# Diagonal of the attention matrix: VectorE sums and two transfers in place of products with ones on TensorE

## The chip, the cores and the metric

The kernel runs on one core of a Trainium2 chip. The engines named below are TensorE (PE; its weight loads are listed apart as PEld), VectorE (DVE), ScalarE (ACT), GpSimd (POOL) and SyncE (SP), whose queue issues the transfers. The metric is the device time of one execution in microseconds (us); the time of a version is the median of its runs.

## The reference

Input x has 32 batches of 512 nodes with 128 features; adj is a 512 x 512 matrix, mostly zeros. Four graph layers follow each other, each as x = x + layer(relu(layernorm(x)), adj). Only the first layer is touched:

```
h0 = h @ W[0];  h1 = h @ W[1]
m  = adj > 0
A  = softmax(where(m, e[cumsum(m) - 1], -9e15), axis=1)      # 512 x 512
M  = eye(512)
out = (A * M) @ h0 + (A * (1 - M)) @ h1 + bias
```

So the attention matrix A is split into its diagonal, which scales the rows of h before a product with W[0], and the rest, which multiplies h W[1]. The layers behind it (two Chebyshev hops, a message layer, a dense attention) only take part as the work that fills the rest of the time.

## The kernel before, in words

The 512 nodes lie as NT = 4 tiles of 128 partitions. The order of the instructions on PE, DVE, ACT and POOL is written out by hand: from line 166 to line 1148 they run in source order on each engine. Transfers on SP are placed by the tile framework, except where the source asks for program order. Within an engine, an instruction that waits holds up all those behind it.

The opening stage, some 40 us, builds A row tile by row tile (t = 0 to 3). `score_rows(t)` makes the scores on PE (lines 625 and 629). `softmax_rows(t)` adds and minimises them on DVE (636, 637) and exponentiates on ACT (638), `inverse(t)` takes the reciprocal on DVE (642), and `scaled_rows(t)` writes the scaled row tile into `att` on ACT (645). The columns inside a row tile are stored in a crossed order (32-wide pieces), which `split` and `crossed` undo. Of each row tile, the 128 x 128 block on the diagonal is called `own`. POOL multiplies it by the identity into `diag` (648) and subtracts that from `own` (649), so `att` holds A without its diagonal.

PE then transposes `att` (line 475) into four PSUM banks `p_attT`; ACT and DVE copy them out in halves (line 316), and `att_sums` builds from them, on DVE, the sums of a Strassen-like scheme of seven half-size products (lines 331 to 335). The right operands are `g`, the projected h W[1] (PE 435, copies 460), and its differences `rt_g`, made on POOL (356).

`round0(r)` does the first layer for two pairs of batches, r = 0 to 7. It runs the seven products on PE (line 386, banks p_l_a, p_l_c, p_l_d) and does other work between them: statistics on DVE (227, 233, 235, 236), normalisation on ACT (247), transposes of h (265, copies 268), later done by DVE and transfers (283, 290, 292). The diagonal part is added by `straight_block` (line 759), which multiplies `hd` by W[0] into the same banks. `hd` is made on POOL by `straight` (line 703): the feature-major h times `adiag`, a 128 x 512 tile whose every partition holds the 512 diagonal values, so that a column scaling becomes an elementwise product.

`adiag` is made once, in round 0 after the second product: `ones`, a 128 x 128 tile of ones, multiplies `diag` on PE, tile by tile (828), which sums each column of `diag` over partitions and leaves the sum on every partition; ACT copies the bank out (829). `adiag` stays in use for the whole first layer.

Of the kernel before, what the change touches and what calls it, by code (L numbers as in the profile page):

```python
# [9 lines left out]
F32 = mybir.dt.float32  # L10
# [14 lines left out]
def kernel(  # L25
# [51 lines left out]
    def bank(name):  # L77
        return psum.tile([P, 512], F32, tag="bank", name=name)
# [11 lines left out]
    def crossed(ap):  # L90

        return ap.rearrange("p (a b c) -> p b a c", a=NT, b=NQR)

    def split(ap):
        return ap.rearrange("p (a b c) -> p a b c", a=NT, b=NQR)
# [83 lines left out]
    nc.scalar.activation(prep.tile([P, 1], F32, name="powers"), eps, AF.Exp)  # L179
    minus_half = const.tile([P, NT, 2], F32, name="minus_half")  # L180
    nc.vector.memset(minus_half, -0.5)
    ones = const.tile([P, P], F32, name="ones")
    nc.vector.memset(ones, 1.0)

    known = prep.tile([P, NT, 2], F16, name="known")
    nc.vector.tensor_copy(known[:, :, 1], rows)
# [280 lines left out]
    def go(steps, n=99):  # L467
        for _ in range(n):
            if next(steps, steps) is steps:
                return  # L470
# [145 lines left out]


    diag = prep.tile([P, NT, P], F32, name="diag")
    least = prep.tile([P, NT], F32, name="least")
    total = prep.tile([P, NT], F32, name="total")  # L620

# [19 lines left out]
    def inverse(t):  # L641
        nc.vector.reciprocal(total[:, t : t + 1], total[:, t : t + 1])

    def scaled_rows(t):
        nc.scalar.mul(split(att[:, t, :]), crossed(us[t]), total[:, t : t + 1])
        own = split(att[:, t, :])[:, :, t, :]
        d = diag[:, t, :].rearrange("p (b c) -> p b c", c=QR)
        nc.gpsimd.tensor_mul(d, own, ident.rearrange("p (b c) -> p b c", c=QR))
        nc.gpsimd.tensor_sub(own, own, d)

    attT = square_tile("attT")
# [12 lines left out]
    softmax_rows(2)  # L664
    inverse(1)
    scaled_rows(1)
    score_rows(3)
    next(turned[1])
    next(turned[1])
    softmax_rows(3)  # L670
    inverse(2)
    scaled_rows(2)
    go(early_stats_2, 2)
    inverse(3)
    scaled_rows(3)
    next(project[1])
    pt = [bank(f"p_attT_{j}") for j in range(NT)]
    transpose_rows(pt, att, 0)
    transpose_rows(pt, att, 1)
    go(project[1])  # L680
    left_of_att = att_sums()
    next(left_of_att)
    att_copies((0, 0, nc.scalar.copy), (1, 0, nc.vector.tensor_copy),
# [37 lines left out]

    ahead = {q: stats_steps(q) for q in range(4, NQ)}
    ln3 = stats_steps(3)
    own, turning, hd, adiag = {}, {}, {}, []
    sums_ahead = late_sums()

    def normalise(q):
# [34 lines left out]
    def round0(r):  # L762

        now = rights.pop(r)
        if r == 0:

            adiag.append(work.tile([P, N], F32, tag="rt", name="adiag", bufs=6))
            p_adiag = bank("p_adiag")  # L770
        A, C = 2 * r, 2 * r + 1

        def x_of(I, b):
            return x_block(r, I, b)

        def diagonal(p, I, b, first):
            straight_block(p, lambda w: hd[A + w, b], I, w0[:, 0, :], first)

        u = [u_tile(f"l0_{r}_{i}") for i in range(3)]
        held = {}  # L780

        def evict(k, p):
            pv = halves(p)
            if k == 1:
                nc.vector.tensor_add(tiles(u[0].rearrange("p i e -> p (i e)")), tiles(p), spread(b0, NT))
            elif k == 6:
                nc.vector.tensor_add(u[1], pv, u[0])
            elif k == 5:
                held["d"] = pv
            elif k == 7:  # L790
                nc.vector.tensor_add(u[2], pv, u[0])
                nc.vector.tensor_add(u[2], held["d"], u[2])
            elif k == 2 and r == 0:
                held["a"] = p
            elif k == 2:
                upper(p)
            elif k == 4:
                diagonal(p, 1, 0, False)
                nc.vector.tensor_add(x_of(1, 0), of_pairs(pv), x_of(1, 0))
            elif k == 3:  # L800
                diagonal(p, 0, 1, False)
                nc.vector.tensor_add(x_of(0, 1), of_pairs(pv), x_of(0, 1))

        def upper(p):
            diagonal(p, 0, 0, False)
            nc.vector.tensor_add(x_of(0, 0), of_pairs(halves(p)), x_of(0, 0))

        def add(I, b, i):
            nc.gpsimd.tensor_add(x_of(I, b), x_of(I, b), of_pairs(u[i]))

        more = r + 1 < NQ // 2
        nothing = iter(())
        stats_a, stats_c = ahead.get(A + 5, nothing), ahead.get(C + 5, nothing)
        own_a, own_c = own.pop(A - 2, nothing), own.pop(C - 2, nothing)
        for i, _ in enumerate(products(f"l0_{r}", by_token, sums["att"], now, evict,
                                          ORDER if r else ORDER0)):
            if r == 0:
                if i == 0:
                    transpose_rows(pt, att, 2)
                    transpose_rows(pt, att, 3)  # L820
                    att_copies((0, 1, nc.scalar.copy), (1, 1, nc.vector.tensor_copy))
                    next(left_of_att)
                    next(left_of_att)
                    go(early_stats_2)
                    att_copies((2, 1, nc.scalar.copy), (3, 1, nc.scalar.copy))
                elif i == 1:
                    for t in range(NT):
                        nc.tensor.matmul(p_adiag[:, blk(t)], ones, diag[:, t, :], start=True, stop=True)
                    nc.scalar.copy(adiag[0], p_adiag)  # L829
                    go(normal[2], NT + 1)  # L830
                    diagonal_of(0, 0)
                    go(ln3, NT + 1)
                    go(normal[2])
                    next(left_of_att)
                    next(left_of_att)
                    next(squares)
                    go(ln3)
                elif i == 2:
                    diagonal_of(0, 1)
                    add(1, 0, 0)  # L840
                elif i == 3:
                    next(turned[2])
                    go(turned[2])
                    add(0, 1, 1)
                    bias(0)
                    normalise(3)
                    go(ahead[4], NT)
                    go(squares)
                elif i == 4:
                    upper(held["a"])  # L850
                    turned.append(pe_steps(h[3], "hT0_3", hT[3]))
                    next(turned[3])
                    go(ahead[4])
                    add(1, 1, 2)
                    go(turned[3])
                    go(projection(2))
                    normalise(4)
                    go(ahead[5], NT)
                    bias(1)
                    go(turn(4))  # L860
                    go(ahead[5])
                elif i == 5:
                    go(projection(3))
                    go(right_of(1))
                    diagonal_of(1, 0)
                    normalise(5)
                elif i == 6:
                    go(stats_c, NT)
                continue
            if i == 0:  # L870
                if C + 2 < NQ:
                    go(turn(C + 2))
                if A + 4 < NQ:
                    normalise(A + 4)
                diagonal_of(r, 1)
                add(1, 0, 0)
            elif i == 1:
                add(0, 1, 1)
                go(stats_a, NT + 1)
                go(own_a, NT)  # L880
                if more:
                    bias(r + 1)
                go(stats_a)
                go(own_a)
            elif i == 2:
                if more:
                    go(projection(A + 2))
            elif i == 3:
                add(1, 1, 2)
                if not more:  # L890
                    next(next_layer)
                if C + 4 < NQ:
                    normalise(C + 4)
                if r >= 3:
                    go(sums_ahead, 2)
            elif i == 4:
                if A + 4 < NQ:
                    go(turn(A + 4))
            elif i == 5:
                if more:  # L900
                    go(projection(C + 2))
                    go(right_of(r + 1))
                    diagonal_of(r + 1, 0)
                go(stats_c, NT + 1)
                go(own_c, NT)
            elif i == 6:
                go(stats_c)
        p = bank(f"p_l0_{r}_e")
        diagonal(p, 1, 1, True)
        nc.vector.tensor_add(x_of(1, 1), of_pairs(halves(p)), x_of(1, 1))  # L910
        if r == 0:
            go(stats_c)
        go(own_c)
        own[A], own[C] = stats_steps(A), stats_steps(C)
        if r + NQ // 4 < NQ // 2:
            loads(r + NQ // 4)
# [279 lines left out]
```

## Time and profile before

| | |
|---|---|
| time, median of 3 runs | 964.42 us (964.27 to 965.08) |
| profiled span | 962.7 us |
| PE busy | 953.7 us |
| DVE, ACT, POOL busy | 585.3, 470.1, 421.7 us |
| products with ones, line 828 | 8 instructions of 275 ns, starting from 34.2 to 34.9 us |
| copy of adiag, line 829 | 587 ns, at 35.3 us |
| POOL product and difference of the diagonal, 648 and 649 | 4 of 459 ns and 4 of 457 ns, from 24.7 to 30.1 us |
| first use of adiag, line 703 | POOL, at 35.9 us |

The page of a profile lists busy time by engine, then the chain of work that ended last, followed back from the last instruction through whatever released each step. A row of the timeline gives the start, the duration, the engine, the line, the operation with its output and inputs, a count, and in brackets how long the engine had been idle and what ended that. A row of the chain gives the start, the duration on the chain and the piece of work. Names carry no buffer numbers.

### The profile page before, as it was taken

How to read it: one execution, taken by the hardware profiler on the slowest of the kernel's cores; microseconds unless marked ns; L12 is line 12 of the kernel's file. 1: busy time of each engine (PE TensorE's matmuls, PEld its weight loads, DVE VectorE, ACT ScalarE, POOL GpSimd, SP SyncE). 2: the span in 40 equal slices, each digit the busy share in tenths (PEclk: the TensorE clock that was granted, in tenths of full speed). 3: DMA queues.
4: the chain of work that ended last, by engine and by line, in shares of the span. 5: the costliest groups of instructions: out<-in, count | busy, mean ns of one | idle time of the engine just before them, and what ended most of it. 6: DMA issues, size and time to landing. Idle time of an engine off the chain costs nothing.

```text
span 962.7 us, 15161 instructions
## 1 busy us (share of the span) xinstructions
PE 953.7 (99%) x5469; PEld 780.9 (81%) x5469; DVE 585.3 (61%) x1332; ACT 470.1 (49%) x1055; POOL 421.7 (44%) x463
## 2 busy tenths in 40 slices
PE   8999999999999999999999999999999999999998
PEld 4899999898989989899878777777677777767776
DVE  8878885846536546657667665665654444444444
ACT  5865452442232233277627654444765445544553
POOL 4878987833517522512333444433032233223322
PEclk9999999999999999999999999999999999999999
DMA  9256533341341231343333423233131121211111
GB/s 253 60 157 192 155 110 88 95 114 55 104 138 41 70 84 27 110 110 92 85 105 99 127 88 88 70 86 88 55 89 55 55 77 44 76 57 45 55 33 44
DMA packets 83913, 86.04 MB, mean 89 GB/s; under 512 B 6784, under 2 KB 74624, under 8 KB 83840
## 3 DMA queue, kind: packets, MB, share of 16 engines
q1 hardware_dynamic: 83840, 85.09, 31.8%
q8 instruction: 43, 0.70, 0.3%
q14 instruction: 30, 0.25, 0.1%
HBM read 44.17 MB, written 40.89 MB: 88 GB/s over the span
## 4 chain that ended last, share of the span: by engine, by line
PE 96%; ACT 2%; DMA 1%; DVE 1%; SPq 0%; issue 0%; DVEq 0%; ACTq 0%
PE p_av L1116 12%; PE p_score L1101 11%; PE p_l_c L386 8%; PE p_w L435 6%; PE p_l_d L386 5%; PE p_msgT_c L379 5%; PE p_l_a L386 4%; PE p_x1T_c L379 4%; PE p_l L435 3%; PE p_feat L435 3%; PE p_hv L435 3%; PE p_msgT_d L379 3%; PE p_msgT_a L379 3%; PE p_phi L1071 3%; PE p_qkh L1088 3%; PE p_phi L1072 3%
## 5 line engine op out<-in xcount | busy, mean ns | idle before, releaser
L247 ACT ACTIVATE h<-x,sh,rs 128x128 f32<-128x128 f32 x512 | 209.6, 488 | 51.2 <-PE p_x1T_d L379 21.7
L1106 POOL TENSOR_TENSOR ex<-ex,adjTx 128x512 f32<-128x512 f32 x62 | 80.5, 1298 | 208.1 <-ACT ex L1104 208.1
L1102 ACT ACTIVATE ex<-p_score 128x512 f32<-128x512 f32 x128 | 71.9, 587 | 122.8 <-issue 113.0
L1116 PEld LDWEIGHTS p_av<-qkh_hv,ex 128*128 128x128 f32 x1024 | 118.4, 191 | 8.4 <-issue 7.4
L1116 PE MATMUL p_av<-qkh_hv,ex 128*128 128x129 f32 x1024 | 119.9, 274 | 0.0
L1101 PE MATMUL p_score<-qkh_hv,hT 128*128 128x512 f32 x256 | 115.2, 593 | 0.0
L283 DVE STREAM_TRANSPOSE hb_hT<-h 128x512 f32<-128x512 f32 x120 | 82.0, 698 | 23.7 <-ACT h L247 23.4
L1106 DVE TENSOR_TENSOR ex<-ex,adjTx 128x512 f32<-128x512 f32 x66 | 46.2, 703 | 81.7 <-ACT ex L1104 81.7
L227 DVE BATCH_NORM_STATS2 bn<-x 128x6 f32<-128x256 f32 x248 | 89.7, 417 | 0.6
L1101 PEld LDWEIGHTS p_score<-qkh_hv,hT 128*128 128x128 f32 x256 | 46.2, 190 | 46.5 <-issue 44.7
L1104 ACT ACTIVATE ex<-ex 128x512 f32<-128x512 f32 x128 | 76.7, 630 | 1.9
L356 POOL TENSOR_TENSOR rt_feat<-feat,feat 128x256 f32<-128x256 f32 x16 | 11.6, 727 | 136.0 <-ACT feat L1055 136.0
L949 ACT COPY w<-p_w 128x512 f32<-128x512 f32 x32 | 18.3, 577 | 106.0 <-PE p_w L435 106.0
L356 POOL TENSOR_TENSOR rt_w<-w,rt_w 128x512 f32<-128x512 f32 x16 | 20.4, 1276 | 110.4 <-DVE rt_w L356 92.1
L435 PE MATMUL p_w<-th,x1T 128*128 128x128 f32 x256 | 49.5, 275 | 0.0
L435 PE MATMUL p_w<-th,hs 128*128 128x128 f32 x256 | 49.5, 275 | 0.0
L435 PEld LDWEIGHTS p_hv<-vw,hT 128*128 128x128 f32 x256 | 33.6, 192 | 15.3 <-issue 8.1
L1066 POOL TENSOR_TENSOR x<-x,phi2b 128x256 f32<-128x256 f32 x64 | 44.5, 730 | 0.0
L435 PEld LDWEIGHTS p_w<-th,hs 128*128 128x128 f32 x256 | 39.9, 192 | 0.7
L1055 ACT ACTIVATE feat<-feat 128x512 f32<-128x512 f32 x32 | 20.2, 632 | 41.3 <-DVE feat L1054 41.3
L1121 DVE SCALAR_TENSOR_TENSOR x<-p_av,rsum,x 128x128 f32<-128x128 f32 x128 | 39.1, 347 | 1.9
L703 POOL TENSOR_TENSOR hd<-hT,adiag 128x512 f32<-128x512 f32 x32 | 39.7, 1275 | 0.3 <-ACT adiag L829 0.3
(234 smaller groups left out, 2039.0 us busy)
## 6 DMA issues: line engine op xcount, KB each, us to landing
d_hT<-hb_hT SPq DMA_DIRECT2D x240, 128.0 KB
hT<-d_hT SPq DMA_DIRECT2D x60, 512.0 KB
x<-in_x_dram SPq DMA_DIRECT2D x32, 256.0 KB
out_dram<-x SPq DMA_DIRECT2D x31, 256.0 KB
adj_s<-in_adj_dram SPq DMA_DIRECT2D x4, 256.0 KB
adjT_d<-adj_squares SPq DMA_DIRECT2D x4, 256.0 KB
sq<-in_adj_dram SPq DMA_DIRECT2D x4, 256.0 KB
adjTx<-adjT_d SPq DMA_DIRECT2D x4, 256.0 KB
```

The source lines that it names most:

```text
L227: nc.vector.bn_stats(st[:, k].rearrange("p e s -> p (e s)"), xt[q][:, b, t : t + 2, :].rearrange("p t f -> p f t"))
L247: nc.scalar.activation(h[:, b, t, :], xt[q][:, b, t, :], AF.Relu, bias=shift[q][:, i : i + 1], scale=scale[q][:, i : i + 1])
L283: nc.vector.transpose(hb[:, :, b].rearrange("p j t r -> p t j r"), h[:, b].rearrange("p t (j c) -> p t j c", c=QR))
L379: nc.tensor.matmul(p[:, :H], b[:, k, :], a[:, k, :], start=(first and k == 0), stop=(k == 1), skip_group_check=True)
L386: nc.tensor.matmul(p[:, i * 2 * D : (i + 1) * 2 * D], a[:, k, blk(i)], b[:, k], start=(first and i == 0 and k == 0), stop=(k == 1), skip_g ...
L435: nc.tensor.matmul(p[:, blk(t)], hT(t), w, start=(i == 0), stop=(i == len(terms) - 1))
L1066: tc.keep_in_program_order(nc.gpsimd.tensor_add(xi, xi, spread(phi2b, 2)))
L1101: nc.tensor.matmul(ps, hT[:, t, b, :], qkh, start=True, stop=True)
L1102: nc.scalar.activation(ex[:, t, :], ps, AF.Tanh, scale=1.0 / (8.0 * math.sqrt(D)))
L1104: nc.scalar.activation(ex[:, t, :], ex[:, t, :], AF.Exp, scale=8.0)
L1106: eng.tensor_mul(split(ex[:, t, :]), split(ex[:, t, :]), crossed(adjTx[0][:, t, :]))
L1116: nc.tensor.matmul(po[:, i, : D + 1], ex[:, t, blk(i0 + i)], hv[:, t, :], start=(t == 0), stop=(t == NT - 1))
```

## The change

The diagonal values are now taken by DVE. A fused multiply and reduce over the free dimension writes `diag` (own times identity) and, in the same instruction, its row sum, which is the diagonal element of that row, into one column of `diag_of` (128 x 4). POOL keeps only the subtraction. The four calls are spread through the opening stage as `without_diagonal(t)`. A first transfer writes `diag_of` to 512 consecutive words in DRAM, a second reads those words back to all 128 partitions as `adiag`. Both stand in program order on SP, before the attT copies. PE's products with ones, the bank they used, ACT's copy and the `ones` tile are gone. `adiag` is allocated earlier, ahead of the `rt_g` tiles of round 0. The aim is to take work from PE and ACT that other parts of the chip can do.

```
-    ones = const.tile([P, P], F32, name="ones")
-    nc.vector.memset(ones, 1.0)
...
+    diag_of = prep.tile([P, NT], F32, name="diag_of")
...
     def scaled_rows(t):
         nc.scalar.mul(split(att[:, t, :]), crossed(us[t]), total[:, t : t + 1])
+
+    def without_diagonal(t):
+
         own = split(att[:, t, :])[:, :, t, :]
         d = diag[:, t, :].rearrange("p (b c) -> p b c", c=QR)
-        nc.gpsimd.tensor_mul(d, own, ident.rearrange("p (b c) -> p b c", c=QR))
+        nc.vector.tensor_tensor_reduce(d, own, ident.rearrange("p (b c) -> p b c", c=QR), 1.0, 0.0,
+                                       OP.mult, OP.add, diag_of[:, t : t + 1])
         nc.gpsimd.tensor_sub(own, own, d)
...
     softmax_rows(2)
     inverse(1)
     scaled_rows(1)
+    without_diagonal(0)
     score_rows(3)
...
     softmax_rows(3)
+    without_diagonal(1)
     inverse(2)
     scaled_rows(2)
     go(early_stats_2, 2)
     inverse(3)
     scaled_rows(3)
     next(project[1])
+    without_diagonal(2)
     pt = [bank(f"p_attT_{j}") for j in range(NT)]
     transpose_rows(pt, att, 0)
     transpose_rows(pt, att, 1)
-    go(project[1])
+    next(project[1])
+    without_diagonal(3)
+    next(project[1])
+
+    adiag = [work.tile([P, N], F32, tag="rt", name="adiag", bufs=6)]
+    diag_d = bounce.tile([N], F32, tag="diag", name="diag_d", bufs=1)
+    tc.keep_in_program_order(nc.sync.dma_start(diag_d.rearrange("(t p) -> p t", p=P), diag_of))
+    tc.keep_in_program_order(nc.sync.dma_start(
+        adiag[0], bass.AP(tensor=diag_d.tensor, offset=diag_d.offset, ap=[[0, P], [1, N]])))
     left_of_att = att_sums()
...
-        if r == 0:
-
-            adiag.append(work.tile([P, N], F32, tag="rt", name="adiag", bufs=6))
-            p_adiag = bank("p_adiag")
...
                 elif i == 1:
-                    for t in range(NT):
-                        nc.tensor.matmul(p_adiag[:, blk(t)], ones, diag[:, t, :], start=True, stop=True)
-                    nc.scalar.copy(adiag[0], p_adiag)
                     go(normal[2], NT + 1)
```

More of the change, by code (lines that the diff above doesn't have):

```diff
@@ L723 @@
     ln3 = stats_steps(3)
-    own, turning, hd, adiag = {}, {}, {}, []
+    own, turning, hd = {}, {}, {}
     sums_ahead = late_sums()
```

## The prediction

> **What bounds the kernel now.** I read the page first: engines, then the chain.
>
> ```profile
> PE 953.7 (99%) x5469; PEld 780.9 (81%) x5469; DVE 585.3 (61%) x1332; ACT 470.1 (49%) x1055; POOL 421.7 (44%) x463
> ...
> PE 96%; ACT 2%; DMA 1%; DVE 1%; SPq 0%; issue 0%; DVEq 0%; ACTq 0%
> ```
>
> TensorE is busy for 99% of the span and holds 96% of the chain that ended last. Every operation that the diff touches lies, by the view of the tile diag, between 24.7 and 35.3 us (its products with ones at 34.2, their copy at 35.26), apart from the readers of adiag, which begin at 35.9. So only a stretch of some twenty microseconds matters, and what comes out of it shifts all the rest. The chain of waits in time order shows that stretch:
>
> ```profile
> 27.93 1.23 ACT att L645 x2
> 29.16 0.36 ACT attT L316
> 29.52 0.04 issue
> 29.56 1.99 PE p_l_a L386 x8
> 31.55 0.87 PE p_attT L475 x8
> 32.43 1.90 PE p_l_a L386 x8
> 34.33 0.91 PE p_adiag L828 x8
> 35.24 0.02 issue
> 35.26 0.02 ACT adiag L829
> 35.28 0.46 issue
> 35.74 2.04 ACT h L247 x5
> ...
> 40.23 3.09 ACT h L247 x8
> 43.32 0.04 issue
> 43.36 0.33 PE p_hT L265
> 43.69 1.79 PE p_g L435 x16
> ```
>
> See two things. The products with ones are on the chain (0.91 us), and so is the copy behind them: ACT begins the third normalisation at 35.74 because of it. From 35.74 to 43.3 the chain is ACT, not PE; from 43.36 on it is PE without a gap until 181 us. The result is therefore the shift of the moment 43.36, carried to the end. The timeline of DVE shows what stands where the new instructions go:
>
> ```profile
> 27.96 0.16 DVE L642 RECIPROCAL total<-total 128x1 f32<-128x1 f32 x1
> 28.05 1.27 DVE L460 COPY g<-p_g 128x512 f32<-128x512 f32 x2
> 29.25 0.42 DVE L316 COPY attT<-p_attT 128x256 f32<-128x256 f32 x1
> 29.59 0.75 DVE L227 BATCH_NORM_STATS2 bn<-x 128x6 f32<-128x256 f32 x2
> ```
>
> DVE has no gap here, and its attT copy ends at 29.67, when PE's first p_l_a products, started at 29.56, come to need it (their second instruction pair reads the block that DVE copies).
>
> [...] the reduce of line 637 shows 0.69 us, [...] the four d_hT transfers issued from 50.08 show data from about 50.8 to 53.3, and the dependent issue begins at 53.98. No row of before shows a transfer of 4-byte elements that I can time.
>
> **The change, part by part.**
>
> Removed from PE: 8 instructions of p_adiag, 0.91 us on the chain. Removed from ACT: one copy of 0.59 us and a wait of 1.52 us before it. Without them ACT's next instruction waits for sh of line 236, which ends at 34.42 in the old trace, 1.32 us before 35.74. The ones memset (0.17 us at 0.9) is followed by a wait for POOL's rows, so it was hidden. POOL loses 4 products of 0.46 us; these lie beside other work, since its rt_g operations also wait for DVE's copies of g (ended 29.32).
>
> Added to DVE: four reduces with their accumulator reads. By start-to-start times of line 637 (22.25, read at 22.87, next at 22.94) overlap takes 0.07 us off and the read adds 0.07, so I take 0.29 us each, bounded by 0.22 (read free) and 0.6 (as slow as the 512-wide one).
> - Row 0 stands behind the reciprocal of 24.43 and waits for ACT's att (ends 24.58). It pushes the hT copy from 24.65 to 24.91 and the score operation to 25.52, which ends at 26.2; the next reduce waits for PE until 26.38 anyway. The idle 0.38 us there hides it.
> - Row 1 moves inverse(2) from 27.00 to about 27.4; ACT wants it at 27.84 behind its exponential. Hidden.
> - The two statistics and inverse(3) then end at 28.28, ahead of ACT's fourth row at 28.45. Hidden.
> - Row 2 needs att row 2, which ACT ends at 28.56. DVE waits from 28.3 to 28.58 and goes on at 28.87; behind it stand the first copy of g (0.6, to 29.47), row 3 (to 29.76; its att ended at 29.16), the second copy of g (to 30.36), and the attT copy, which ends at 30.78 in place of 29.67: 1.11 us later. That is the price.
>
> PE begins p_l_a at 29.56 as before, does two instructions, waits until 30.82, and does the other six at 0.216 us (1.73 for 8): it ends at 32.12, and the transposes begin then in place of 31.39: +0.73. Everything behind carries +0.73 on PE and DVE until the p_adiag slot, where 0.89 us (start to start, 34.17 to 35.06) is saved: p_l_c begins at 34.90 in place of 35.06, the next transposes (38.52 before) at 38.36. PE gains 0.16.
>
> ACT: sh of line 236 ends at 34.42 + 0.73 = 35.15, so normalisation starts at 35.17 in place of 35.74, and its eight instructions and the square root (its statistics end at 36.5, in time) end at 38.57. The copies of hT need PE's first four transposes, 38.36 + 0.5 = 38.86 (before, 39.15, ACT-bound); the second follows at 39.36, and the next normalisation begins at 39.88 in place of 40.11 to 40.23, ending 0.25 us earlier. With it 43.36 becomes about 43.1. **Sum: -0.25 us.**
>
> Added transfers: SP issues nothing between 24.8 and 41.65 us, and all 16 engines idle from about 28 to 42, so nothing is queued behind. The first waits for row 3's read at 29.85. From the d_hT row: 0.8 us from issue to data, 0.65 from last data to the next issue. 512 pieces of 1 KB took 2.5 us there, so for 512 pieces of 4 bytes I take 0.6 to 2.5, say 1.5. The second: 0.8 to data, 256 KB at 180 to 350 GB/s (rates seen at d_hT) 0.7 to 1.4[...]. adiag lands at 29.95 + 0.8 + 1.5 + 0.65 + 0.8 + 1.1 + 0.5 = 35.3, between 34.3 and 36.6. POOL ends its rt_g work at about 35.7 and reaches hd then (35.92 before), so the wait is at most about 0.9 us. Who waits: PE's p_l_a L759 at 41.1 needs the first two hd (2.5 us after the start, slack 2.7), and behind hd stand POOL's additions, whose last frees DVE at 44.63, then ACT's normalisation at 45.99, then its copies of g (end 50.5) and POOL's rt_g (second ends 53.2), wanted by PE at 55.12: slack about 2 us. A landing up to 37.8 costs nothing.
>
> **The rivals.**
> 1. All of PE's share is gained: the reduces pair away without moving the attT copy, as their low bound and some slack would allow. Then PE is 0.89 us earlier, ACT starts at 34.44: about 0.9 saved, 963.5. For it: PE is 96% of the chain. Against: DVE shows no gap from 27.0 to 30.95.
> 2. The reduces cost about 0.6 each: the first two spill past the idle 0.38 us by some 0.5, the last two push the copy by 0.6 more; 43.36 moves by about +0.9, 965.3. For it: this is a custom operation whose 128-wide form the trace lacks.
> 3. The new wait is the transfers: 4-byte writes at three times the 1 KB pieces' time, so that adiag lands near 40.2. Then 2.4 us lie beyond the slack and, as the path is in order from POOL to PE, come through, less the 0.25: 966.6. For it: 512 scattered elements. Against: 512 larger pieces took 2.5 us.
>
> **How the numbers follow.** The forecast (shift of -0.25, from 964.42 to 964.2) gets 0.58, rival 1 0.19, rival 2 0.12, rival 3 0.08; 0.03 is left for an effect late in the kernel in my favour. The bound of 0.2% is 1.93 us: the forecast and rivals 1 and 2 lie within it, rival 3 outside. PE's whole saving of 0.9 with its stalls between 28 and 43 us (1.73 + 1.73 + 3 x 0.87 or so of work in 8.3 us of chain leave about 0.5, and 0.3 near 29.3) is under 1.93, so faster beyond it is nearly shut out: faster 0.04, same 0.86, slower 0.10. The range takes in rivals 1 and 2: 963.1 to 965.6.
>
> **What would show it.** In the profile after: PE has 8 matmuls fewer; line 316's DVE copy starts near 30.4, and PE shows a wait of about 0.8 us inside the first p_l_a; ACT has no wait of 1.5 near 35; its normalisation starts near 35.2; POOL's first hd starts within 0.5 us of 35.9, and PE's p_g (43.5 before) stands near 43.3 in the same count. If PE's first p_l_a runs through, rival 1 holds; if the reduce rows read 0.5 us or more, rival 2; if POOL waits for adiag beyond 38, rival 3. The prediction is wrong if a wait appears after 45 us that has no row in the old trace, since everything rests on the shift being carried unchanged.

## The result, and the profile after

The change makes the kernel slower: 972.26 us (971.60 to 973.05, 6 runs) against 964.35 us, a ratio of 1.0081 (95% interval 1.0068 to 1.0094), 7.9 us more. The forecast was 964.2, with a range up to 965.6. Of the cases that the prediction worked out, the one that came true is rival 3, given a chance of 0.08, and it came in more than three times as large as it was worked out.

Line numbers after the change differ by -2 to +14. The page of the changed kernel first: engines, the row of the granted TensorE clock, the chain by engine.

```profile
PE 956.3 (99%) x5461; PEld 782.4 (81%) x5461; DVE 586.8 (61%) x1339; ACT 469.3 (48%) x1054; POOL 419.4 (43%) x459
...
PEclk9899999999999999999999999999999999999999
...
PE 93%; DVE 3%; DMA 2%; ACT 1%; issue 0%; SPq 0%; POOL 0%; DVEq 0%; ACTq 0%
```

PE has its 8 matmuls fewer and yet 2.6 us more busy time; one slice of the clock row is under 9. The totals say no more. The waits do: first those of SP's queue up to 60 us, then those of the engines from 20 to 70 us (who waited, for what; us in total, times, longest).

```profile
SPq L693 <- DMA diag_d<-diag_of: 10.0, 1, 10.0
```

```profile
DVE x L816 <- POOL x L443: 8.8, 1, 8.8
POOL hd L717 <- DMA adiag<-diag_d: 8.2, 1, 8.2
...
PEld p_l_a L773 <- POOL hd L717: 4.3, 2, 3.6
PE p_l_a L773 <- POOL hd L717: 3.6, 2, 3.2
```

The whole line of causes is there. SP waits 10.0 us for the 2 KB write before it may issue the spread; POOL waits 8.2 us for adiag, and what stands behind hd in its order comes later with it (the additions of u at 48.26, before at 40.86); PE waits 3.6 us for hd, and DVE 8.8 for POOL's bias addition behind hd. The timeline dates them (start, duration, engine):

```profile
29.47 0.38 SPq L692 DMA_DIRECT2D diag_d<-diag_of  x1
...
39.96 0.32 SPq L693 DMA_DIRECT2D adiag<-diag_d  x1
...
43.38 4.92 POOL L717 TENSOR_TENSOR hd<-hT,adiag 128x512 f32<-128x512 f32 x4 [8.17 <-DMA adiag<-diag_d]
44.69 0.50 PEld L773 LDWEIGHTS p_l_a<-w,hd 128*128 128x128 f32 x2 [3.58 <-POOL hd L717]
```

What did the write do in the 10.5 us from its issue to that of the spread? The transfer view of 29.3 to 40 us, in 40 slices of 0.27 us, shows its packets (528 packets under 512 bytes on queue q1; the later 7 is one packet, which the view lists under the kind instruction):

```profile
DMA  0000720000000000000007000000000000000000
...
DMA packets 529, 0.01 MB, mean 1 GB/s; under 512 B 528, under 2 KB 528, under 8 KB 528
```

By this view the packets moved within about 0.6 us, near 30.6; the transfer that waits for them was issued 9 us later. The row of transfer activity alone does not show this wait; the queue's own wait does.

The idle PE has a second effect, in the table by stretch (stretch, length, busy PE, PEld, DVE, ACT, POOL, clock, DMA share, GB/s):

```profile
42.00:43.00 1.00, 0.00 (x0) 0.00 (x0) 0.96 (x2) 1.00 (x4) 0.00 (x0) 1.00 0.51 122
43.00:44.00 1.00, 0.00 (x0) 0.00 (x0) 0.23 (x1) 0.04 (x1) 0.62 (x1) 0.80 0.91 184
44.00:45.00 1.00, 0.31 (x1) 0.31 (x2) 0.00 (x0) 0.00 (x0) 1.00 (x2) 0.50 0.93 173
...
49.00:50.00 1.00, 1.00 (x7) 1.00 (x6) 0.00 (x0) 0.62 (x2) 1.00 (x2) 0.50 0.00 0
50.00:51.00 1.00, 1.00 (x9) 1.00 (x9) 0.00 (x0) 0.20 (x1) 1.00 (x2) 0.79 0.00 0
```

PE is idle from 41.5 us, and after about two microseconds of it the granted clock falls to 0.5 and stays there for nearly 7 us. The 0.5 lasts from about 43.6 to 50.4 (worked out from the means of these rows): some 2.1 us of idleness came before the fall, and some 4.5 us of work without a gap, from 45.91 on, before the rise.

At the end of all this PE's p_g of 67.25 us (before) begins at 74.27, 7.02 later; the profiled executions differ by 7.1.

### The profile page after: what moved, and what is told of

Its sections match the earlier page's. It is cut to its first block, busy times and chain, and to the rows that moved or that the text cites. A ratio compares the mean times of both kernels' runs of the same rounds, so it can differ in the third digit from the quotient of the medians.

```text
span 969.8 us, 15152 instructions
## 1 busy us (share of the span) xinstructions
PE 956.3 (99%) x5461; PEld 782.4 (81%) x5461; DVE 586.8 (61%) x1339; ACT 469.3 (48%) x1054; POOL 419.4 (43%) x459
## 4 chain that ended last, share of the span: by engine, by line
PE 93%; DVE 3%; DMA 2%; ACT 1%; issue 0%; SPq 0%; POOL 0%; DVEq 0%; ACTq 0%
PE p_av L1123 12%; PE p_score L1108 11%; PE p_l_c L384 8%; PE p_w L433 6%; PE p_l_d L384 5%; PE p_msgT_c L377 4%; PE p_x1T_c L377 4%; PE p_l_a L384 4%; PE p_l L433 3%; PE p_feat L433 3%; PE p_hv L433 3%; PE p_qkh L1095 3%; PE p_x1T_a L377 3%; PE p_msgT_d L377 3%; PE p_x1T_d L377 3%; PE p_msgT_a L377 3%
## 5 line engine op out<-in xcount | busy, mean ns | idle before, releaser
L1108 PEld LDWEIGHTS p_score<-qkh_hv,hT 128*128 128x128 f32 x256 | 46.2, 190 | 46.5 <-issue 44.5
```

The lines of the kernel that those rows point to most:

```text
L1108: nc.tensor.matmul(ps, hT[:, t, b, :], qkh, start=True, stop=True)
```

## The experiments

Each group of runs on one chip had its own runs of the kernel before (964.4 to 964.9 us in the median). Times are medians; a ratio is estimated from all runs and can differ a little from the quotient of the medians.

**e1: the reduces without the transfers.** `ones`, the products and ACT's copy come back; DVE's reduces stay, the two transfers go.

```
-    tc.keep_in_program_order(nc.sync.dma_start(diag_d.rearrange("(t p) -> p t", p=P), diag_of))
-    tc.keep_in_program_order(nc.sync.dma_start(
-        adiag[0], bass.AP(tensor=diag_d.tensor, offset=diag_d.offset, ap=[[0, P], [1, N]])))
...
+                    for t in range(NT):
+                        nc.tensor.matmul(p_adiag[:, blk(t)], ones, diag[:, t, :], start=True, stop=True)
+                    nc.scalar.copy(adiag[0], p_adiag)
```

> The change with its reduces on VectorE, but adiag made again by the products with ones and ScalarE's copy; no transfers. Theory (the time is lost in the wait for the transfers): the reduces alone push PE by the 0.4 us that the transposes of att show in the changed kernel (31.83 in place of 31.39), so 964.4 to 965.2. Rival (VectorE, in order, is what costs): the loss stays, 970 to 972.

Measured: 965.18 us, ratio 1.0005 (0.9997 to 1.0014). VectorE's part costs some 0.7 us by the medians, not told from none; the loss comes with the transfers. The rival falls.

**e2: 128 runs of 16 bytes.** diag_of is contiguous per partition, so the order (p t) in DRAM writes 4 words at a time; POOL then reads adiag with a stride.

```
-    tc.keep_in_program_order(nc.sync.dma_start(diag_d.rearrange("(t p) -> p t", p=P), diag_of))
+    tc.keep_in_program_order(nc.sync.dma_start(diag_d.rearrange("(p t) -> p t", p=P), diag_of))
...
-            nc.gpsimd.tensor_mul(split(s), src, split(scale))
+            nc.gpsimd.tensor_mul(split(s), src, scale.rearrange("p (b c a) -> p a b c", a=NT, b=NQR))
```

> The change, with the diagonal written to DRAM as 128 runs of 16 bytes instead of 512 single words, and read back in that order. Theory 1 (the landing time of the first transfer grows with the number of pieces): its wait of 10.0 us falls to about 3 to 4 us, adiag lands near 36.5, and the time is the one forecast for the change, 963.8 to 964.8. Theory 2 (a fixed delay of a DRAM write that is read at once, or many writers of one line): the wait stays near 10 us and so does the time, 971 to 973.

Measured: 965.73 us, ratio 1.0016 (1.0007 to 1.0024). The wait is gone, as SP's queue shows:

```profile
29.94 0.33 SPq L692 DMA_DIRECT2D diag_d<-diag_of  x1
31.36 0.32 SPq L693 DMA_DIRECT2D adiag<-diag_d  x1
```

1.42 us from issue to issue in place of 10.5. A fixed delay of a write that is read at once is excluded. The time is still 0.9 above the expected range: POOL's hd starts without a wait, but four of them take 6.03 us in place of 4.98 with the strided operand, so its additions come later.

**p1 and p2: the write by itself.** Chains of small transfers behind the end of the kernel before, each waiting for the one before: a write, and its reading back, which waits on SP's queue for the write (9.4 us for d_words_a in p1). The row of the second therefore dates the landing of the first.

```
+        keep(nc.sync.dma_start(view(d), s))
+        keep(nc.sync.dma_start(back, view(d)))
```

> The kernel before, with a chain of small transfers added at its end, each waiting for the one before: the 2 KB of the diagonal's size written to DRAM as 512 single words next to each other (twice), as 128 runs of 16 bytes (three times), as 512 single words 64 bytes apart and 512 bytes apart, as 128 runs of 16 bytes 512 bytes apart, each read back in the same form; then 128 single words, a spread of 512 bytes to all partitions, and two copies within SBUF. Theory 1 (the number of pieces sets the landing): all forms of 512 words take about 10 us, the runs 3 to 4 us. Theory 2 (neighbouring words written by many engines hold each other up): only the 512 words next to each other take 10 us, those 512 bytes apart 3 to 4 us. The time of the kernel itself says nothing.

> The kernel before with another chain of dependent small transfers at its end: 512 single words written to DRAM next to each other, then 2, 4, 8 and 16 words apart, next to each other again; 512 single words into every second word of an SBUF tile; then 128 runs of 1, 2 and 4 words next to each other. Theory 2a (words of two engines in the same 64 bytes hold each other up): only the words next to each other (both times, 10 us) and the 128 runs of one word (7 us) are slow, those 2 apart take under 2.5 us. Theory 2b (the number of part writes to the same 64 bytes counts): 10 us falls step by step with the distance, 2 apart about 5, 4 apart about 3. Into SBUF under 2.5 us by both. The time of the kernel itself says nothing.

Each chain ran once, so every figure is one reading. Measured, in us from the issue of the write to the issue of the transfer that waits for it:

| write, DRAM unless said | us |
|---|---|
| 512 words next to each other (p1 twice, p2 twice) | 9.87, 10.42; 10.16, 8.28 |
| 512 words, 2 apart (p2) | 4.69 |
| 512 words, 4 apart (p2) | 3.07 |
| 512 words, 8 apart (p2) | 2.32 |
| 512 words, 16 apart, 64 bytes (p1, p2) | 1.79, 2.01 |
| 512 words, 512 bytes apart (p1) | 1.97 |
| 128 runs of 4 words, next to each other (p1 twice; p2 last) | 1.45, 1.41; 1.43 |
| the same as the first of each chain, behind the output's stores | 2.21, 2.26 |
| 128 runs of 4 words, 512 bytes apart (p1) | 1.41 |
| 128 runs of 2 words, next to each other (p2) | 2.93 |
| 128 single words, next to each other (p1, p2) | 7.20, 7.19 |
| 512 words into every second word of an SBUF tile (p2) | 2.07 |

The two pairs of rows that matter most (p1; d_lines is the form with 64 bytes from word to word):

```profile
964.05 0.37 SPq L1183 DMA_DIRECT2D d_words_a<-probe  x1
973.92 0.37 SPq L1185 DMA_DIRECT2D probe<-d_words_a  x1
...
984.76 0.36 SPq L1183 DMA_DIRECT2D d_lines<-probe  x1
986.55 0.36 SPq L1185 DMA_DIRECT2D probe<-d_lines  x1
```

Theory 1 falls: the same 512 words take 10 us or 2 us by their distance, and a quarter of the words, still neighbours, takes 7.2. Of the second pair, 2b fits better: the delay falls step by step (4.7, 3.1, 2.3, 2.0), where 2a wanted all under 2.5. Every second word of an SBUF tile took 2.07 us where every second word in DRAM took 4.69; words next to each other in SBUF were not tried. From 64 bytes on the delay no longer falls: 2.01 (p2) and 1.79 there, 1.97 at 512 bytes (p1). Why neighbours land late no run shows, and whether it matters which of the 16 engines write them was not separated.

**e6: the change with a write of another form.** One 32x32 block transpose on VectorE turns the 128x32 tile that holds diag_of, and four transfers of 4 runs of 128 bytes write it in node order. Spread and hd stay.

```
+    nc.gpsimd.memset(diag_of, 0.0)
...
+    nc.vector.transpose(diag_on, diag_of)
...
-    tc.keep_in_program_order(nc.sync.dma_start(diag_d.rearrange("(t p) -> p t", p=P), diag_of))
+    for b in range(NQR):
+        tc.keep_in_program_order(nc.sync.dma_start(
+            diag_d.rearrange("(t b c) -> b t c", b=NQR, c=QR)[b], diag_on[b * QR : b * QR + NT, :]))
```

> The change, with the diagonal turned on VectorE by one 32x32 block transpose (128x32), so that it is written to DRAM by four transfers of 4 runs of 128 bytes each, in node order; the spread and hd stay as in the change. Theory (single neighbouring words make the write slow): the last of the four lands some 1.5 us after its issue, the spread is issued near 32.3, adiag lands near 35.7, hd starts at most 0.3 us later than before, and the time is about the one forecast, 963.9 to 964.9. Rival (any write that is read back at once, or VectorE's place in the order): 966 or more.

Measured: 964.98 us, ratio 1.0003 (0.9995 to 1.0012), 0.1 above the theory's range. SP issues the four from 30.27 and the spread at 32.59; POOL shows no wait for adiag:

```profile
34.71 1.27 POOL L354 TENSOR_TENSOR rt_g<-g,rt_g 128x512 f32<-128x512 f32 x1
35.94 4.97 POOL L722 TENSOR_TENSOR hd<-hT,adiag 128x512 f32<-128x512 f32 x4
```

Apart from the block transpose and the clearing of its tile, only the form of the write differs from the change, and the loss is gone.

**e5: how much lateness of POOL is free.** The kernel before, with one unused product on POOL ahead of hd, or, in the second kernel, two.

```
                     nc.scalar.copy(adiag[0], p_adiag)
+                    late_by = work.tile([P, N], F32, tag="rt", name="late_by", bufs=6)
+                    for _ in range(1):
+                        nc.gpsimd.tensor_mul(late_by, att[:, 0, :], att[:, 1, :])
```

> The kernel before, with one product of 128x512 more on GpSimd (1.28 us, result unused) ahead of the first hd, which then starts about 1.0 us later. Theory (the chain from GpSimd's additions over VectorE, ScalarE and the hT transfers to PE's p_g near 67 us has only about 0.2 us of slack): 965.0 to 965.5. Rival (the slack of 2 us that the prediction worked out): 964.2 to 964.6.

> The same with two such products, so that hd starts about 2.3 us later. Theory: 966.2 to 966.8. Rival (slack of 2 us): 964.4 to 964.8.

Measured: 966.10 (964.21 to 967.58, 21 runs; ratio 1.0013, 1.0007 to 1.0020) and 966.90 us (966.30 to 967.78; ratio 1.0022, 1.0013 to 1.0032), each a little above the theory's range. The slack of 2 us is refuted. With two products, PE waits for a row that appears in no list of its waits before:

```profile
PE p_g L435 <- DMA hT<-d_hT: 1.3, 2, 0.8
```

The path is POOL's bias addition, DVE (x, then sh), ACT (normalisation), DVE (block transposes), the d_hT and hT transfers, PE's p_g of round 1. With one product the profiled execution, at 964.55 one of the fastest, shows no such wait: its second group of d_hT transfers was issued 0.85 us later than before, the hT transfer behind them only 0.47 later and the p_g behind that 0.24 later. The runs spread over more than 3 us; I put that down to the transfers' own variation, which no trace shows. The following table sets the start of POOL's additions of u, counted from its first rt_g operation and less the 10.33 us of before, against the time gained or lost. Lateness is from one profile each, the time from the medians.

| kernel | additions later by, us | time, us |
|---|---|---|
| e6 | -0.36 | +0.43 |
| e2 | 0.68 | +1.30 |
| e1 | 0.85 | +0.75 |
| e5, one product | 0.86 | +1.55 |
| e5, two products | 2.23 | +2.35 |
| e3, below | 7.36 | +6.95 |
| after | 7.81 | +7.91 |

Above 2 us it goes about one for one; below 1 us the medians scatter by as much as they tell.

**e3, e8, e10: the clock, and the addition behind hd.** e3 puts filler products where PE idles (first part of the diff); e8 moves POOL's bias addition ahead of the two additions of u (second part; it is taken out behind them); e10 does both.

```
+                    p_fill = bank("p_fill")
+                    for _ in range(5):
+                        nc.tensor.matmul(p_fill, ident, att[:, 0, :], start=True, stop=True)
                     upper(held["a"])
...
                     diagonal_of(0, 1)
+                    bias(0)
                     add(1, 0, 0)
```

> The change, with 5 products of ident and a row tile of att (about 4.3 us of PE work into a bank that nobody reads) put where PE waits for hd. Theory (the gap also halves the granted clock, which costs PE some 2.3 us of work between 45.9 and 50.6): the clock stays at 1.0 and the time falls to 969.6 to 970.6 although PE has more to do. Rival (the clock drop costs nothing, all is the wait): 972 to 973.

> The change, with the same move. Theory (GpSimd's lateness goes on through the addition that waits for the bias: VectorE idled 8.8 us for it and ScalarE's normalisation then started 0.98 us after its last copy of g): ScalarE is now held by its copies alone, about 1 us less, 970.8 to 971.8. Rival (the loss is not passed on through this addition): unchanged, 971.9 to 972.8.

> The change with the bias addition moved ahead and with the five filler products of the earlier run where PE waits for hd. Theory (the clock's fall costs time as soon as GpSimd no longer covers it: with the bias early, ScalarE waits for PE's p_g, which takes 2.9 us at the lower clock in place of 1.8, behind p_hT with 1.7 in place of 0.9): 968.2 to 969.4. Rival (the clock's fall costs nothing here either): 969.6 to 970.6.

e3: 971.38 us, ratio 1.0073 (1.0060 to 1.0085), between the ranges of theory and rival. The clock stays at 1.0 (1.00 from 40 to 50 us, with 4.45 us of filler from 41.93), but the time hardly follows; the interval overlaps that of the change. The theory that the clock costs some 2 us falls: PE is faster at first (p_g at 47.98 in place of 49.06) and then waits for the late engines:

```profile
60.51 1.99 PE L384 MATMUL p_l_c<-rt_g,sums_att 128*128 128x256 f32 x8 [0.93 <-POOL rt_g L354]
...
64.93 2.02 PE L433 MATMUL p_g<-w,hT 128*128 128x128 f32 x16 [0.70 <-DMA hT<-d_hT]
```

e8: 970.01 us, ratio 1.0059 (1.0045 to 1.0073), some 2 us below the change by the medians where 1 was expected, though the two intervals still touch. So a part of the loss goes through the addition that waits for the bias. e10: 970.13 (968.72 to 971.48; ratio 1.0058, 1.0044 to 1.0072), in the rival's range. Its profiled execution, at 968.72 its fastest, has PE without a wait from 45.9 to 76 us and reaches the later p_g at 71.35; that of e8, at 971.31 its slowest, reaches it at 74.08, also without a wait from 46.2 on. The two profiles would speak for the theory, and so would e8 by itself: its three executions at a mean clock of 0.998 took 969.6 to 970.0 us, the two at 0.996 took 970.9 and 971.3. But the medians of e8 and e10 show nothing. What the clock costs once POOL no longer covers it stays open.

**e7 and e9: a version that is not slower.** e7 is the kernel before with the bias addition early. e9 is e6 with it, and with the reduces of rows 2 and 3 behind the copies of g, row 3 also behind the attT copy:

```
-    without_diagonal(2)
     pt = [bank(f"p_attT_{j}") for j in range(NT)]
...
     next(project[1])
+    without_diagonal(2)
+    next(project[1])
+    att_copies((1, 0, nc.vector.tensor_copy))
     without_diagonal(3)
-    next(project[1])
+    nc.vector.transpose(diag_on, diag_of)
...
-    att_copies((0, 0, nc.scalar.copy), (1, 0, nc.vector.tensor_copy),
-               (2, 0, nc.scalar.copy), (3, 0, nc.scalar.copy))
+    att_copies((0, 0, nc.scalar.copy), (2, 0, nc.scalar.copy), (3, 0, nc.scalar.copy))
```

> The kernel before, with GpSimd's addition of the bias to x moved ahead of its two additions of u (from behind them). Theory (in the kernel before, ScalarE's normalisation of 45.99 is held by its own copies of g and not by GpSimd): no change, 964.1 to 964.8. Rival (GpSimd holds the path there already): 962.5 to 963.5.

> The four-block form of the change with the same move, and with the reduces of rows 2 and 3 behind VectorE's copies of g, and the reduce of row 3 behind its attT copy too. Theory: PE keeps more of the 0.9 us of the removed products, as its wait in the first p_l_a goes, and a later hd no longer matters: 963.4 to 964.2. Rival (the hT transfers and ScalarE set the path, so that PE's saving is not seen): 964.3 to 965.0.

e7: 964.31 us, ratio 0.9997 (0.9989 to 1.0005): no change. e9: 963.79 us, ratio 0.9992 (0.9984 to 1.0000), 0.8 below the 964.62 of its neighbours. PE's first p_l_a now runs without its gap, and the products behind it follow closely:

```profile
29.73 1.99 PE L384 MATMUL p_l_a<-g,attT 128*128 128x256 f32 x8
31.56 1.04 PE L473 MATMUL p_attT<-ident,att 128*128 128x128 f32 x8
32.50 1.99 PE L384 MATMUL p_l_a<-g,attT 128*128 128x256 f32 x8
34.33 1.89 PE L384 MATMUL p_l_c<-rt_g,sums_att 128*128 128x256 f32 x8
```

It is the fastest version measured. The 0.8 us is close to the 0.9 that p_adiag had on the chain, but the interval reaches to no change, and no run tells apart what its edits give.

## Why the prediction was wrong

**Right in part: where it would be decided.** The change acts on the opening, and from the later p_g on the shift is carried unchanged to the end (7.02 there, 7.1 in the span). Before that it is not, though the prediction carried it from 43.36 on. PE's p_g of 43.52 moved by 5.54 (to 49.06); the p_l_c of 45.31, behind that p_g at the lower clock (2.60 us in place of 1.95), by 6.19 (to 51.50); the later p_g by 7.02, behind a wait for hT that has no row in the old trace. Such a wait was the prediction's own sign of being wrong.

**Right in the main: the reduces and the attT copy.** The row of the new operation, and the copy that it pushes:

```profile
29.15 0.28 DVE L650 CUSTOM_DVE_ANT_0 diag<-att,ident 128x128 f32<-128x128 f32 x1
29.36 0.08 DVE L650 DVE_READ_ACCUMULATOR2_ANT diag_of<- 128x1 f32 x1
29.36 0.69 DVE L458 COPY g<-p_g 128x512 f32<-128x512 f32 x1
...
29.96 0.41 DVE L314 COPY attT<-p_attT 128x256 f32<-128x256 f32 x1
30.43 1.56 PE L384 MATMUL p_l_a<-g,attT 128*128 128x256 f32 x6 [0.38 <-DVE attT L314]
```

The operation shows 0.28 us and its read 0.08, and the copy starts 0.21 us after the operation did; I took 0.29 for both, an estimate (the old trace's operations on two inputs, 0.69 us for 512 columns in line 637 and 0.41 for 256 in 335, give 0.27 for the operation). This execution is 0.29 us ahead before the change acts (the last reduce of line 637 ahead of it starts at 23.53, before at 23.82). With that, p_l_a resumed at 30.43 where I had 30.82, that is 0.1 early; the transposes at 31.83 (32.12) and those of h at 38.06 (38.36) stand as worked out. The wait inside p_l_a, said to be about 0.8 us, shows as 0.38 on PE and as 0.78 for its weight loads. ACT's normalisation at 35.27 (35.17) is 0.4 late. So up to the point where hd is needed the forecast held nearly everywhere. e6, in which adiag arrives in time, came out 0.4 us above before by the medians, in an interval that takes in both no change and the forecast's -0.25.

**Wrong: the size of the first transfer.** The step reads "512 pieces of 1 KB took 2.5 us there, so for 512 pieces of 4 bytes I take 0.6 to 2.5, say 1.5". With its 0.8 before and 0.65 behind, I had 2.95 us from issue to dependent issue; it took 10.5. The row I bounded it by showed how fast pieces move, and the packets did move in 0.6 us. The time that I missed lies between the last packet and the dependent issue: some 9 us, where I carried over 0.65 from pieces of 1 KB. The bound from above was no bound: I had no row of the old trace with neighbouring words of 4 bytes as a destination in DRAM. The second transfer took 3.4 us to hd's start, where I had 2.4, with 0.5 from its last data to hd as a bare estimate. One thing in this step was off before any run: the low terms sum to 34.0 and not 34.3, which would not have saved the forecast.

**Wrong: the slack of 2 us.** I followed one path from POOL, through ACT's copies of g to PE's use of rt_g, and found 2 us. e5 shows that another, over the block transposes and the hT transfers, gives out earlier: POOL 0.86 us late cost 1.55 in the median, 2.23 late cost 2.35. The rows of this transfer, before and then after:

```profile
63.75 0.34 SPq L292 DMA_DIRECT2D hT<-d_hT  x1
67.25 2.05 PE L435 MATMUL p_g<-w,hT 128*128 128x128 f32 x16
...
70.82 0.34 SPq L290 DMA_DIRECT2D hT<-d_hT  x1
74.27 2.05 PE L433 MATMUL p_g<-w,hT 128*128 128x128 f32 x16 [0.54 <-DMA hT<-d_hT]
```

In the old trace PE took hT 3.50 us after its issue. Where PE had to wait for it, that took 3.45 (after) and 3.33 (e5 with two products), so by these three executions the slack was only 0.05 to 0.2 us. The row at 63.75 was there to be read. One link of this path shows as no wait at all: VectorE's small sh ahead of the normalisation ends with the rt_g operation that POOL has running. It took 0.40 us and ended at 55.70, rt_g at 55.67, before; 1.30 us, at 62.80 and 62.77, after; with POOL idle an sh took 0.17 us (57.32, after). If POOL holds VectorE here, the rt_g of the path that I did follow also delays the path that I did not; that is a reading of these rows, and no run tests it.

**Rival 3** had the right mechanism and its sum had these two terms too small: a landing at 40.2 where it was 43.4, and 2 us of slack where there was next to none. The 40.2 also does not follow from its terms: three times 2.5 us in place of 1.5 makes 41.3, and with the slack of 2 a time near 967.7. "For it: 512 scattered elements" was the wrong reason too, since spreading the words out is what made them fast (10 us next to each other, 2.0 at 64 bytes). In the last part, PE's work from 35.06 to 43.36 has three products of 1.73 us, not two; with three the 0.5 us left over comes out.

**The clock** was in no step. It fell to 0.5. With it kept at 1.0 (e3) the median is 0.9 us lower, in an interval that overlaps the change's, so its own part of the loss is not told from none while POOL is late as well.

## What to carry to other kernels

Price a small transfer to DRAM by the landing of a write of the same form, not by how fast pieces move; if the trace has none, measure one by itself before it is put ahead of a path. Single neighbouring words were a bad form here: the same 2 KB in runs of 16 bytes took 1.4 us, and as four transfers with runs of 128 bytes, made by a block transpose, 2.3 us together, in place of 10. When an engine gets a new wait, follow every path that starts with what is queued behind it, the transfers it leads to included, and take the shortest slack.

## What was not expected of the hardware

A 2 KB write whose packets had moved in about 0.6 us let the transfer that waits for it go only some 9 us later; spacing the words 64 bytes apart brought 10 us down to 2.0. An SBUF destination at every second word took 2.07 us, DRAM at every second word 4.69. A strided fp32 operand (every fourth word) made four of GpSimd's 128x512 products take 6.03 us (e2) in place of 4.98 (before).
